# A graph kernel on one core: another order for the four long neighbour lists, and TensorE at two thirds of its clock in the plan

## The chip, the cores and the metric

The kernel runs on one core of one Trainium2 chip. The metric is the device time of one execution in microseconds (us); lower is better. Times inside an execution count from the first instruction of the profiled one.

## The reference, cut to what matters

There are 16 graphs of 1024 nodes with 64 channels and a dense, weighted adjacency matrix each.

```python
# layer 0
h = maximum(layernorm(x), 0)
x = x + matmul(adj / clip(sum(adj, axis=2), 1), h)
# layer 1
h = maximum(layernorm(x), 0)
adj_d = dilate(adj)          # of a node with over 10 neighbours every skip-th one is removed, both ways
for tau, wt in zip([.25, .5, .75], [.25, .5, .25]):       # per node and channel, over h of its neighbours and itself
    agg += wt * interpolated_quantile(h[neighbours(adj_d)], tau)
y = relu((h + agg) @ W1 + b1) @ W2 + b2
x = x + y * mask
```

The numbers of neighbours differ much: a few nodes have many, most have few.

## The kernel before, in words

**Layer 0** takes the 16 graphs one by one: adjacency rows come in by DMA, TensorE transposes them and multiplies, and VectorE (DVE) finds up to 32 neighbours of each row from the signs. Each node's record (channels of layer 1, residual, neighbours) is scattered to the table `srt` of its group, sorted by the number of neighbours. A group is four graphs; there are four groups. `tab` holds a group's channels, `whole` a copy of all groups' tables.

**Layer 1** works on jobs. A job (`Job`) is 128 nodes by T columns whose lists have the same number of places. The lists up to 15 places are the short jobs, by class, of each group (tiles `places`, four buffers). The 512 nodes with the longest lists, 8 of each graph for each of four lengths, are four **long lists** of 128 nodes: 88, 31, 24 and 20 places (`LONG`; called list 88, list 31, list 24, list 20 below). A job goes through these steps:

1. For a long list only, in `long_lists`: its records come by the SP queue (`lS`), GpSimd (POOL) gathers the nodes' adjacency rows (`lat`), and DVE **selects** the neighbours from them: the key of each place, the segments' largest by MAX8 and MATCH_REPLACE8, and from them the row numbers `lidx`.
2. POOL **gathers** one place of 128 nodes at a time by an indirect DMA: `places<-tab,idx` for a short job, `lplaces<-whole,lidx` for a long list. So list 88 takes 88 gathers, list 20 takes 20.
3. The **head**: DVE compares for removed neighbours (`rem`, `gone`, `ok`, `valid`, `q`, `wu`; with an l in front for a long list). `rem` needs all gathers of the job.
4. ScalarE (ACT) adds a huge number to removed places (`places<-places,gone`), one operation a place.
5. DVE **sorts** the places by a network of minima and maxima between `places` and `other` (for a long list between `lplaces` and `long_other`).
6. DVE forms the weights (`w`, `lw`), ACT or DVE multiplies.
7. TensorE (PE) sums the products (`pt`), and the two matrix products of the layer follow over ACT (`ot`, `hid`) and PE (`ps_small`); DVE adds the residual (`y`).
8. POOL scatters the **output** `out_dram<-y`, 128 nodes at a time. For long lists its row numbers are `lnodes_i`; for the short jobs of the last group they are `last_nodes_i`.

List 88 has its own buffer `lplaces0`. The other three lists share two buffers `lplaces`: the third of them can be gathered only when the first has been summed by PE.

**The order.** DVE and POOL are scheduled by hand. Each stream of work is a Python generator that yields before each step what engine it needs and when its inputs are ready by the plan's clocks. `Plan.run` takes the stream that could begin first by these clocks, and among equals the lowest rank. `Plan.note` adds each instruction's cost to the plan's clock of its engine. What `Plan.run` chose is written into the engine's queue, and the engine then follows that queue in order. The loop over the long lists gives each a rank, so that the first one's gathers come ahead of the next one's:

```python
        for l, K in enumerate(LONG):
...
            job = Job(
                pool, n, 1, keys, idx.unsqueeze(1), node, mask, nodes_i, whole, S, NG,
                *(("lplaces", 2) if l else ("lplaces0", 1)), -600 + l, begin=at(whole),
            )
            plan.add(job.run(), 100 * NG + l)
```

The cost of a matmul in the plan is 0.1 us and 0.88 ns for each column of its output, twice as much for float32. All instructions of the plan are recorded by one helper, so the profile gives one line, L228, for nearly all of them; they are told apart by their tiles.

Of the kernel before, what the change touches and what calls it, by code (L numbers as in the profile page):

```python
# [39 lines left out]
LONG = (88, 31, 24, 20)  # L40
# [179 lines left out]
class Timed:  # L220


    def __init__(self, plan, name, engine):
        self._plan, self._name, self._engine = plan, name, engine
# [9 lines left out]
class Plan:  # L234
# [4 lines left out]
    def __init__(self, nc):  # L239
        names = {"vector": "DVE", "scalar": "ACT", "tensor": "PE", "gpsimd": "POOL", "sync": "SP"}  # L240
        self.nc = SimpleNamespace(
            **{attr: Timed(self, name, getattr(nc, attr)) for attr, name in names.items()}
        )
        self.clock = dict.fromkeys([*names.values(), "DMA"], 0.0)
        self.ready, self.used, self.users = {}, {}, {}
        self.slots, self.streams = {}, []
        self.last = self.own = None
        self.parts = set()

    def tile(self, pool, shape, dtype, name, bufs, users=0):  # L250

        res = pool.tile(shape, dtype, name=name, bufs=bufs)
        self.slots.setdefault(name, []).append(res.tensor.name)
        self.users[res.tensor.name] = users
        return res
# [12 lines left out]
    def at(self, *tiles):  # L268
        return max(self.ready.get(t.tensor.name, INF) for t in tiles)

    def note(self, engine, op, args, kwargs):
        if self.own is not None:
            self.clock[engine] = max(self.clock[engine], self.own)
        out = kwargs["out"] if "out" in kwargs else args[0]
        rest = [*args[0 if "out" in kwargs else 1:], *(v for k, v in kwargs.items() if k != "out")]
        rest = [getattr(v, "ap", v) if type(v).__name__.startswith("Indirect") else v for v in rest]
        rest = [v for v in rest if isinstance(v, bass.AP)]
        size = max(math.prod(v.shape[1:]) for v in (out, *rest[:2]))
        start = max(
            self.clock[engine],  # L280
            *(self.ready.get(v.tensor.name, 0.0) for v in rest if self.own is None),
            self.used.get(out.tensor.name, 0.0) if self.own is None else 0.0,
        )
        after = 0.15
        apart = engine == "SP" and out.tensor.name in self.parts
        if apart:
            start = max(self.clock[engine], *(self.ready[v.tensor.name] for v in rest))
        if engine == "DVE":
            half = op == "tensor_tensor" and all(v.dtype == HF for v in (out, *rest))
            time = 0.04 if op == "memset" else 0.07 + size * (0.57e-3 if half else 1.04e-3)  # L290
        elif engine == "ACT":
            pointers = sum(isinstance(kwargs.get(k), bass.AP) for k in ("bias", "scale"))
            time = 0.06 + size * 0.86e-3 + 0.11 * pointers + 0.09 * ("accum_out" in kwargs)
        elif engine == "PE":
            time = 0.1 + math.prod(out.shape[1:]) * 0.88e-3
            if op == "matmul" and rest[0].dtype == F32:
                time *= 2
        elif engine == "POOL":
            time, after = (1.27, 2.2) if op == "indirect_dma_start" else (0.15, 0.1)
            self.last = None  # L300
        else:
            start = max(start, self.clock["DMA"])
            busy = math.prod(out.shape) * 4 / 165e3

            time, after = 0.05, 2.2 + busy * (1 if 4 * out.shape[-1] >= 512 else 2)
            self.clock["DMA"] = start + busy
        self.clock[engine] = end = start + time
        if not apart:
            self.ready[out.tensor.name] = end + after
        for v in rest:  # L310
            self.used[v.tensor.name] = max(self.used.get(v.tensor.name, 0.0), end + after)
        if "accum_out" in kwargs:
            self.ready[kwargs["accum_out"].tensor.name] = end + after
        return start
# [22 lines left out]
def kernel(  # L337
# [27 lines left out]
    with tc.manual_schedule(engines={mybir.EngineType.DVE, mybir.EngineType.Pool}):  # L365
        list_path(tc, x, adj, nodemask, w1, b1, w2, b2, out, go)
# [7 lines left out]
def list_path(ctx, tc, x, adj, nodemask, w1, b1, w2, b2, out, go):  # L374
# [7 lines left out]
    NG = len(GROUPS)  # L382
# [101 lines left out]
    whole = dram.tile([B * TS, W], F32, name="whole")  # L484
# [11 lines left out]
    plan = Plan(nc)  # L496
    plan.parts.update(tab.tensor.name for tab in tabs)
    nc = plan.nc
    new, free, room, at = plan.tile, plan.release, plan.room, plan.at
# [739 lines left out]
    def long_lists(pool):  # L1239
# [1 line left out]
        yield "DVE", always  # L1241
        rev = new(pool, [P, N], HF, "rev", 1)
        nc.vector.tensor_scalar(rev, col_f, -1.0, float(N), op0=OP.mult, op1=OP.add)
        for l, K in enumerate(LONG):
            n = K + 1
            yield "SP", always
            S = new(pool, [P, 1, RW], F32, "lS", 4)
# [62 lines left out]
            for e in range(2):  # L1310
# [7 lines left out]
            yield "DVE", lambda: 0.0 if progress["groups"] == NG else INF  # L1318
            job = Job(
                pool, n, 1, keys, idx.unsqueeze(1), node, mask, nodes_i, whole, S, NG,  # L1320
                *(("lplaces", 2) if l else ("lplaces0", 1)), -600 + l, begin=at(whole),
            )
            plan.add(job.run(), 100 * NG + l)

    progress = {"batches": 0, "begun": 0, "groups": 0, "ahead": 0, "jobs": [0] * (NG + 1)}
    for g in range(NG - 1):
# [1 line left out]
    with tc.tile_pool(name="lay0", bufs=2) as pool:  # L1328

        for stream, first in (  # L1330
            (endings, 0), (channels, 1), (products, 2), (transposes, 4), (listing, 5),
            (beginnings, 6), (loads, 7), (signs, -15),
        ):
            now = [0]
            plan.add(stream(pool, now), lambda first=first, now=now: 10 * now[0] + first)
        plan.run(lambda: progress["batches"] == B)
    with tc.tile_pool(name="long", bufs=1) as pool:

        plan.add(group(NG - 1, pool, "last_"), -2000)
        plan.add(long_lists(pool), -1500)  # L1340
        plan.run()
# [292 lines left out]
```

## Time and profile before

| | |
|---|---|
| median of 3 runs | 1513.86 us (1511.95 to 1516.6) |
| the profiled execution | 1512.82 us, of which its span 1511.0 |
| DVE busy | 1191.3 us, 79% of the span |
| POOL busy | 957.2 us, 63% |
| ACT busy | 816.4 us, 54% |
| PE busy | 738.8 us, 49% |
| gathers of long lists | 163, 1.03 us each |
| last record of layer 0 scattered | at about 889 us |

A busy share is an average over the whole execution, in which layer 0 and layer 1 overlap until about 889 us. For the part after that the stretches of the profile are to be read. POOL's gathers are counted busy while their DMA is prepared, not during the short pause to the next, so a full POOL queue shows as some 75%.

### The profile page before, as it was taken

Reading aid. Unit: us, or ns where it says so; the run is one execution under the profiler, and the core shown is the slowest. Engines: PE = TensorE matmul, PEld = TensorE weight load, DVE = VectorE, ACT = ScalarE, POOL = GpSimd, SP = SyncE. Lnnn points to the kernel's source line nnn. Section 1 sums busy time; section 2 is a strip of 40 time slices with the busy share of each in tenths; the row PEclk is TensorE's granted clock in tenths of the full one; section 3 lists DMA queues with packets and bytes.
Section 4 is the critical chain, followed back from the end, with each engine's and each line's share of the span. In section 5 each row is a group of like instructions: output and inputs, shape, how many; then the busy total and the mean of one; then the engine's idle time right before and its main releaser. Section 6 shows DMA issues by size and latency. Waiting matters only on the chain. (4 is left out here: it accounts for less than half of the span.)

```text
span 1511.0 us, 15983 instructions
## 1 busy us (share of the span) xinstructions
PE 738.8 (49%) x3192; PEld 464.7 (31%) x3192; DVE 1191.3 (79%) x4104; ACT 816.4 (54%) x2789; POOL 957.2 (63%) x1154
## 2 busy tenths in 40 slices
PE   4778777327877556567667620024000123228542
PEld 2434334214544233343444320012000122216432
DVE  6777798997899779859869869893059999986875
ACT  7989878557879457757975520201050223148341
POOL 0122227777678757757777787667777777765083
PEclk8889888658888777869688755555555565558765
DMA  5445665424355253355341242111111111211010
GB/s 177 150 142 168 163 210 160 123 73 114 101 162 152 59 174 94 99 126 161 94 140 31 60 101 68 50 37 28 30 26 23 28 28 40 44 33 22 2 25 13
DMA packets 135718, 133.36 MB, mean 88 GB/s; under 512 B 100756, under 2 KB 103444, under 8 KB 135492
## 3 DMA queue, kind: packets, MB, share of 16 engines
q1 hardware_dynamic: 102876, 90.79, 20.8%
q0 software_dynamic: 32736, 41.47, 11.2%
q14 instruction: 78, 0.64, 0.1%
q8 instruction: 28, 0.46, 0.1%
HBM read 112.90 MB, written 23.61 MB: 90 GB/s over the span
## 5 line engine op out<-in xcount | busy, mean ns | idle before, releaser
L228 POOL DMA_INDIRECT places<-tab,idx x372 | 370.2, 995 | 131.7 <-issue 101.8
L228 PE MATMUL pt<-ident,prod 128*128 128x128 f32 (+1 forms) x736 | 160.2, 377 | 517.8 <-DVE prod L228 241.2
L228 PEld LDWEIGHTS pt<-ident,prod 128*128 128x128 f32 (+1 forms) x736 | 129.3, 256 | 550.4 <-ACT prod L228 412.4
L228 PE MATMUL ps_small<-att,h 128*65 128x512 f32 x512 | 254.7, 644 | 27.3 <-ACT h L228 10.5
L228 POOL DMA_INDIRECT srt<-row,to x128 | 125.9, 984 | 165.8 <-ACT row L228 144.0
L228 PE MATMUL pt<-ident,at 128*128 128x128 f32 x1024 | 176.7, 320 | 96.0 <-ACT att L228 71.1
L228 POOL DMA_INDIRECT lplaces<-whole,lidx x163 | 167.2, 1026 | 55.6 <-issue 48.5
L228 DVE MAX8 rec<-sg 128x8 f16<-128x256 f16 x512 | 180.1, 414 | 4.4
L228 PEld LDWEIGHTS pt<-ident,at 128*128 128x128 f32 x1024 | 136.9, 164 | 143.5 <-ACT att L228 93.8
L228 ACT ACTIVATE sg<-at 128x1024 f16<-128x1024 f32 x128 | 134.8, 1054 | 75.0 <-DMA at<-in_adj_dram 65.7
L228 ACT COPY att<-pt 128x512 f32<-128x512 f32 x256 | 141.9, 582 | 20.7 <-PE pt L228 18.8
L228 POOL DMA_INDIRECT places<-tab,last_idx x124 | 123.8, 998 | 41.3 <-issue 35.0
L228 PEld LDWEIGHTS ps_small<-att,h 128*65 128x65 f32 x512 | 74.7, 151 | 161.9 <-issue 123.2
L228 ACT ACTIVATE places<-places,gone 128x64 f32<-128x64 f32 x496 | 123.5, 335 | 0.5
L228 ACT ACTIVATE prod<-places,w 128x64 f32<-128x64 f32 x213 | 54.1, 336 | 120.5 <-DVE w L228 120.5
L228 POOL DMA_INDIRECT out_dram<-y,nodes_i x93 | 91.8, 987 | 22.6 <-issue 15.1
L228 DVE TENSOR_TENSOR sg<-sg,keyed 128x1024 f16<-128x1024 f16 x128 | 87.2, 681 | 23.7 <-ACT sg L228 23.7
L228 ACT ACTIVATE gone<-gone 128x15 f32<-128x15 f32 (+9 forms) x40 | 8.2, 206 | 169.2 <-DVE ok L228 169.0
L228 DVE TENSOR_TENSOR long_other<-lplaces 128x512 f32<-128x512 f32 (+5 forms) x124 | 64.1, 555 | 29.1 <-ACT lplaces L228 28.9
L228 DVE TENSOR_TENSOR other<-places,other 128x64 f32<-128x64 f32 (+6 forms) x204 | 69.6, 341 | 5.9
L228 PE MATMUL ps_small<-ot,w_sb 128*128 128x128 f32 (+3 forms) x112 | 47.6, 513 | 44.2 <-DVE y L228 31.2
L228 DVE TENSOR_TENSOR places<-places,other 128x64 f32<-128x64 f32 (+2 forms) x208 | 62.3, 309 | 4.9
(231 smaller groups left out, 1670.8 us busy)
## 6 DMA issues: line engine op xcount, KB each, us to landing
at<-in_adj_dram SPq DMA_DIRECT2D x128, 512.0 KB
places<-tab,idx POOLq DMA_INDIRECT x372, 2.5
whole<-tab SPq DMA_DIRECT2D x4, 1057.0 KB
tab<-row SPq DMA_DIRECT2D x16, 264.0 KB
xt<-in_x_dram SPq DMA_DIRECT2D x16, 256.0 KB
lplaces<-whole,lidx POOLq DMA_INDIRECT x163, 2.4
srt<-row,to POOLq DMA_INDIRECT x128, 2.7
places<-tab,last_idx POOLq DMA_INDIRECT x124, 2.4
```

The source lines that it names most:

```text
L228: ins = getattr(self._engine, op)(*args, **kwargs)
```

## The change

There are two edits. The long lists are taken in the order 31, 24, 88, 20, and rank follows that order; which buffers a list uses stays (list 88 has `lplaces0`, the others share two). And from the end of layer 0 on, the plan counts each PE instruction 1.5 times as long. Neither edit alters what an instruction computes; both alter the clocks and ranks by which the plan orders the queues after layer 0.

```diff
@@ Plan.__init__
         self.parts = set()
+        self.pace = 1.0
@@ Plan.note
             if op == "matmul" and rest[0].dtype == F32:
                 time *= 2
+            time *= self.pace
@@ long_lists
-        for l, K in enumerate(LONG):
+
+        for nth, l in enumerate((1, 2, 0, 3)):
+            K = LONG[l]
             n = K + 1
...
-                *(("lplaces", 2) if l else ("lplaces0", 1)), -600 + l, begin=at(whole),
-            )
-            plan.add(job.run(), 100 * NG + l)
+                *(("lplaces", 2) if l else ("lplaces0", 1)), -600 + nth, begin=at(whole),
+            )
+            plan.add(job.run(), 100 * NG + nth)
@@ list_path, after layer 0
         plan.run(lambda: progress["batches"] == B)
+    plan.pace = 1.5
     with tc.tile_pool(name="long", bufs=1) as pool:
```

Written out, POOL's queue before has, from the selection of the lists on: the gathers of list 88 with 14 outputs in it, then those of lists 31 and 24 (55), short jobs and outputs, the output of list 88, the gathers of list 20, and outputs. In the changed kernel it has: the gathers of list 31 with 4 outputs in it, those of list 24, those of list 88 with the outputs of lists 31 and 24 in it, those of list 20 with 10 outputs, then short jobs and outputs; the outputs of lists 88 and 20 stand among the last 23.

## The prediction

> **What bounds the kernel now.** I read the slices first, then the stretch that they point to, then what ended each wait there, and last the end of the chain.
>
> ```profile
> DVE  6777798997899779859869869893059999986875
> ...
> POOL 0122227777678757757777787667777777765083
> ```
>
> One digit is 37.8 us. Layer 0 is over at about 890 us, in the 24th slice. POOL (GpSimd) stays at 7: a gather runs 0.94 us and the next starts 0.30 us later, so 7 is a full queue. DVE (VectorE) has one hole, the digits 3 and 0. Table by stretch, DVE being the third pair of columns and POOL the fifth:
>
> ```profile
> 1032.00:1046.00 14.00, 14.00 (x50) 8.96 (x48) 0.08 (x1) 5.68 (x19) 10.49 (x12) 0.58 0.12 27
> 1048.00:1096.00 48.00, 0.00 (x0) 0.00 (x0) 0.00 (x0) 0.00 (x0) 37.90 (x52) 0.50 0.12 29
> 1096.00:1120.00 24.00, 0.00 (x0) 0.00 (x0) 6.42 (x18) 22.10 (x91) 18.20 (x20) 0.50 0.13 27
> 1120.00:1347.00 227.00, 41.08 (x176) 32.48 (x177) 220.00 (x708) 44.92 (x175) 174.42 (x176) 0.55 0.16 33
> ```
>
> DVE does nothing for 48 us while POOL issues 52 entries; then it is busy 97% of 227 us. What ended the hole, and the other long waits from 1000 us on (us in total, times, longest):
>
> ```profile
> POOL out_dram L228 <- DVE y L228: 58.1, 5, 36.2
> ...
> DVE lrem L228 <- DMA lplaces<-whole,lidx: 50.1, 2, 48.9
> ...
> DVE long_other L228 <- ACT lplaces L228: 28.9, 9, 5.7
> ...
> DVE other L228 <- ACT places L228: 13.6, 3, 11.2
> ```
>
> lrem is the first operation on the list of 88; it needs all 88 gathers. The 36.2 us are POOL waiting at 1390.8 to 1427.0 with the output of list 88, and the gathers of list 20 stand behind it:
>
> ```profile
> 1427.05 0.96 POOL L228 DMA_INDIRECT out_dram<-y,lnodes_i  x1 [36.23 <-DVE y L228]
> 1434.22 0.97 POOL L228 DMA_INDIRECT lplaces<-whole,lidx  x1 [6.22 <-PE pt L228]
> ```
>
> In the timeline DVE then sorts list 31 (1394.4 to 1425.4), 24 (1436.0 to 1461.5) and 20 (1470.5 to 1491.2), and nothing comes after. So POOL's gathers bound the stretch to 1096.5, and VectorE's work, with short waits, the rest. TensorE is never the bound here.
>
> **What the Trainium skill says.** PSUM — Partial Sum Buffer, section Engine vs sequencer instructions: the queues of ScalarE, VectorE and GpSimd are strict FIFO. The trace agrees: twenty gathers of list 20 stood behind one output for 36.23 us. SBUF — State Buffer, section Who interferes with whom: a VectorE instruction with two SBUF inputs contends with a GpSimd instruction that reads SBUF. The trace agrees in sign: with VectorE idle the gathers of list 88 start every 1.25 us, while VectorE sorts list 88 (1119 to 1172) 36 of them take 53 us, 1.50 each; with short jobs between, 1.32 (1172 to 1250).
>
> **The change, part by part.** Both parts alter only the order in which the plan writes the queues. Against the kernel before, the queues are the same up to the selection of the first long list (916.3), no instruction but 26 products on ACT in place of two on DVE (about 2 us) and two memsets is added or removed, so what counts is what stands before what. With the new list order alone the GpSimd queue differs from the changed one only in places of outputs (those of lists 31 and 24 stand up to three gathers elsewhere); the clock part is priced at 0, within 4 us. In SP's queue the copy of the last table to `whole` stands three loads earlier; it still starts when the marks are written (927.2 now) and lands before the first long gather (945): 0.
>
> *Selection, up to 1007.* DVE selects 31 first (20.4 us by its rows, from 916.3) and then 24 (19.9). The row of list 24 lands 4.6 us after its issue at 941.4, so DVE starts it at 946.0 and ends at 965.9. The row for list 88 is issued at 966.1; with 5.8 us of small work before it, its selection (35.6) ends at 1007.3. Only then can the row of list 20 be gathered, and POOL, in order, has done all that stands before it at 998.6: it waits 8.9 us. Before, it waited 4.5 and 3.9 at the two like places.
>
> *The gathers, 1007 to 1160.* After that row 114 entries of POOL's queue lead to the last gather of list 88: 22 of list 24, 88 of list 88, one each of lists 20 and a short job, the outputs of 31 and 24. Meanwhile DVE has 20's selection (19.6), two short rests (7.2), list 31 (30.4), 11 us of waiting on ACT as before 1436.0, and list 24 (25.2, ending 1106). At 1.29, 1.33, 1.43, 1.25 and 1.40 us an entry these stretches take 18, 5, 21, 9 and 18 entries (1.43 and 1.40 I chose between the 1.50 above and the 1.35 of 1434 to 1461); the other 42 go at 1.25. From 1008.8 that ends at 1159, and lrem of list 88 starts at **1160.5 in place of 1096.5: 64 us later.** With all at 1.25 it is 1153, with all at 1.39 1169. Neither output should stop POOL: 31's is ready at 1106 and met at about 1116, 24's at 1118 and met at 1137.
>
> *What DVE no longer has after it.* Lists 31 and 24 now lie in front: 31.0 + 25.5 us of the timeline above and 2.5 for their heads, the 59 us that the rows of both queues also differ by. **Minus 59.** So the hole is not filled, it moves: DVE waits from 1106 to 1118 for the output of list 24, which stands ahead of lrem in its queue, and then to 1160 for the gathers, because nothing else has been gathered. The first of these waits costs nothing while the second covers it.
>
> *The middle.* List 88 waits for the first additions on ACT as it does now (17.6 us in five pieces behind 88 additions in 21.1 us). Between it and the end of 88's sort DVE has 17.5 us more of short jobs, which are missing after it: 0. Short jobs' gathers have 4 us or more of slack by the same entries (the closest: 20 gathers of a job needed at 1361, done at 1357); with four buffers for them I leave 2 us for misses. End of sort: 1160.5 + 250.8 + 17.5 + 2 = 1431.
>
> *The tail.* Before, DVE waited after that point 5.1 + 0.8 + 11.2 + 1.6 + 6.0 + 0.7 + 1.3 + 5.7 = 32.4 us. Now ACT has 18 products of a short job, 67 multiplications of list 88, 17 additions and 12 products of short jobs, then the 20 additions of list 20, at 0.24 each, with copies between: some 38 us (ACT's own rows), against 13 us of DVE's work until list 20. By their order in the queues DVE waits 3.5 and 5.5 us before short jobs and 16.2 before list 20: 25. **Minus 7.** Then list 20 sorts for 19.9. After its weights, 10.3 us passed to the last output's data (1491.2 to 1501.5), and one scatter. Now 15 outputs stand behind the same point, at 1.26: 19 us, which cover the 10.3. **Plus 8.**
>
> Sum by differences: 64 - 59 + 2 - 7 + 8 = +8. Counted forward along the new queues: 1431 + 13 of work + 25 of waits + 20 for list 20 + 20 for its weights and the outputs + 8 from the last scatter to the end (as 1503.0 to 1511.0 now) = 1517, +6. The two differ by roundings of the durations; I take the second, whose steps are the measured rows. The profiled execution took 1512.8 with a span of 1511.0 (1.8 around it), and the median of the runs is 1.0 above it: **1520**.
>
> **The rivals.**
> - *A, the hole moves (0.58):* as above, 1520; by the paces of a gather and 3 us either way in the tail 1509 to 1531.
> - *B, ScalarE drains in time (0.22):* the tail is where it is decided. If list 88's multiplications run while DVE still sorts short jobs, the 25 us shrink to 5: 1500, faster. It decides from 11 us on. For it: before 1347 ACT is busy only 45 of 227 us. Against it: the multiplications need weights formed after the sort, as at 1347.3, and their 16 us belong ahead of list 20 in the queue.
> - *C, an output or a buffer stops POOL (0.20):* as the 36.23 us did. A place is the eleven outputs ahead of the 20-gather job, or the wait for one of four short-job buffers; each 10 us that a job's gathers come late beyond the 4 us of slack reach DVE, which has only list 88 to turn to, and whose queue is fixed. Two such waits: 1540.
> - *That it doesn't do what it says* can be only in part: the order of lists is in the queues; the clock's factor could be without effect, which is already inside A.
>
> **How the numbers follow.** A difference under 0.3% (4.5 us) can't be told from none here. A gives slower 0.36, same 0.19, faster 0.03; B faster 0.20, same 0.02; C slower 0.20. Together faster 0.23, same 0.21, slower 0.56. The range takes B's 1500 as its low end and C's 1540 as its high end; beyond lies under 2 in 10.
>
> **What would show it.** In the changed profile: POOL waiting 9 us for the row of list 20 near 1000; list 31 sorted from about 1040; lrem of list 88 at 1153 to 1169 after a wait of 35 to 45 us on its gathers; end of list 88's sort near 1431; DVE waiting on ACT additions before list 20; a row of some 15 outputs at the very end. Wrong would be lrem before 1145, a VectorE without that wait, or a POOL wait over 10 us in front of gathers after 1160.

## The result

The changed kernel took **1520.71 us** (median of 15 runs, 1516.99 to 1528.16) against 1513.86 us of the kernel before in the same rounds: a ratio of 1.0041, 95% interval 1.0027 to 1.0056. The profiled execution took 1520.98 us with a span of 1519.2. So the change makes the kernel slower, by about 7 us, 0.4%.

The experiments ran on four chips. On two of them, called A and B below, the kernel before took 1956 and 1977 us; on the other two, C and D, 1516 and 1517. Times are therefore compared only with the kernel before on the same chip, or as stretches inside one trace.

### The profile page after: what moved, and what is told of

It reads as the page before. It is cut to its first block, busy times and chain, and to the rows that moved or that the text cites. A ratio compares the mean times of both kernels' runs of the same rounds, so it can differ in the third digit from the quotient of the medians.

```text
span 1519.2 us, 15998 instructions
## 1 busy us (share of the span) xinstructions
PE 764.0 (50%) x3192; PEld 478.7 (32%) x3192; DVE 1189.4 (78%) x4102; ACT 824.0 (54%) x2815; POOL 958.9 (63%) x1152
## 5 line engine op out<-in xcount | busy, mean ns | idle before, releaser
L228 PE MATMUL pt<-ident,prod 128*128 128x128 f32 (+1 forms) x736 | 169.2, 392 | 498.2 <-ACT prod L228 295.0
L228 PEld LDWEIGHTS pt<-ident,prod 128*128 128x128 f32 (+1 forms) x736 | 136.6, 269 | 533.7 <-ACT prod L228 407.7
L228 PE MATMUL ps_small<-att,h 128*65 128x512 f32 x512 | 262.7, 661 | 27.6 <-ACT att L228 10.1
L228 POOL DMA_INDIRECT lplaces<-whole,lidx x163 | 163.5, 1003 | 49.7 <-issue 48.4
L228 POOL DMA_INDIRECT places<-tab,last_idx x124 | 127.5, 1029 | 57.2 <-issue 35.0
L228 ACT ACTIVATE prod<-places,w 128x64 f32<-128x64 f32 x239 | 60.5, 336 | 86.1 <-DVE w L228 86.0
L228 DVE TENSOR_TENSOR long_other<-lplaces 128x512 f32<-128x512 f32 (+6 forms) x124 | 63.9, 554 | 40.1 <-ACT lplaces L228 25.5
L228 ACT COPY ot<-pt 128x128 f32<-128x128 f32 (+3 forms) x56 | 22.0, 394 | 110.9 <-PE pt L228 109.2
```

Source lines behind the costliest of these rows:

```text
L228: ins = getattr(self._engine, op)(*args, **kwargs)
```

## The profile after

The slices of the changed kernel, one digit being 38.0 us:

```profile
DVE  6877698997899779869769867999710899999842
POOL 0122227777677767757776787657777876577714
```

The hole of VectorE is still there. Before it was the digits 3 and 0, in the 28th and 29th slice; now it is 7, 1 and 0 in the 29th to 31st. The last slices of VectorE are 8, 4 and 2 and those of POOL 7, 1 and 4: at the end the two wait for each other.

The table by stretch (busy us and number of instructions of PE, PEld, DVE, ACT, POOL, then the granted clock, the DMA share and GB/s). I cut it at the landmarks of the trace: the wait for list 88's gathers, list 88's sort with short jobs in it, the time to list 20's weights, and the rest.

```profile
1116.00:1161.00 45.00, 0.00 (x0) 0.00 (x0) 0.02 (x1) 0.00 (x0) 34.03 (x37) 0.53 0.13 29
1161.00:1429.00 268.00, 62.74 (x243) 47.44 (x244) 242.90 (x773) 82.22 (x324) 195.11 (x208) 0.54 0.14 31
1429.00:1486.00 57.00, 44.28 (x250) 34.94 (x249) 31.25 (x123) 38.37 (x154) 12.63 (x20) 0.77 0.03 8
1486.00:1519.00 33.00, 13.63 (x72) 11.79 (x72) 3.40 (x17) 5.62 (x21) 15.95 (x29) 0.60 0.06 18
```

In 45 us VectorE does one instruction. Then it is busy 91% of 268 us, and in the 57 us to list 20's weights only 55%. In the last row, 33 us, little but outputs is left.

What ended the long waits from 1000 us on (us in total, times, longest):

```profile
POOL out_dram L228 <- DVE y L228: 49.1, 3, 34.1
...
DVE lrem L228 <- DMA lplaces<-whole,lidx: 45.1, 1, 45.1
...
DVE long_other L228 <- ACT lplaces L228: 25.5, 8, 7.8
...
DVE long_other L228 <- PE pt L228: 14.4, 1, 14.4
...
POOL places L228 <- ACT prod L228: 11.4, 2, 11.1
```

The wait of lrem is 45.1 us where it was 48.9. The wait of 14.4 stands before list 20's sort. The end of POOL's timeline:

```profile
1487.17 0.95 POOL L228 DMA_INDIRECT out_dram<-y,last_nodes_i  x1 [34.12 <-DVE y L228]
...
1495.43 0.96 POOL L228 DMA_INDIRECT out_dram<-y,lnodes_i  x1 [5.93 <-DVE y L228]
...
1510.58 0.95 POOL L228 DMA_INDIRECT out_dram<-y,last_nodes_i  x1 [0.19 <-POOLq L370]
```

Fifteen outputs stand in this row. The first starts when VectorE has come past list 20's sort, two are issued, then POOL waits 5.93 us for the output of list 88, and it and the last twelve follow at 1.26 us each.

## The experiments

The theory was the prediction's: POOL's gathers set when list 88 can start, VectorE and its waits set the rest, and the clock part is worth about nothing. The main rival was that the clock part has a cost of its own.

### The new list order alone

```diff
-    plan.pace = 1.5
+    plan.pace = 1.0
```

It ran on three chips: A, B and D.

> The new list order alone, the plan's clock for TensorE unchanged. Theory of the prediction (the hole moves from 1048-1096 to 1116-1161, the clock part is worth 0 within 4 us): lrem of list 88 within 3 us of 1161 after a wait of about 45 us, list 88's sort done at about 1429, time 1520.7 within 4 us (ratio to before 1.002 to 1.007). Rival (the clock part takes back or adds much): over 5 us away from 1520.7. Rival (the order is worth nothing, the clock part made the change): 1513.9.

> The new list order alone once more; on the first chip the kernel before took 1956 us in place of 1514, with pauses of up to 42 us on ACT, DVE and PE that no wait explains, so the size of the effect could not be read there. If this chip is like the one of the changed kernel (before at about 1514): lrem of list 88 within 3 us of 1161 after a wait of about 45 us, list 88's sort done at about 1429, 1520.7 within 4 us. Rival (the clock part takes back or adds much): over 5 us away from 1520.7.

> The new list order alone, on a chip on which before takes about 1516 (if it is the last one again). Theory: lrem of list 88 within 3 us of 1161 after a wait of about 45 us, list 88's sort done at about 1429, ratio to before 1.0033 as the whole change, within 0.003; so the clock part is worth 0 within 4 us. Rival: the order alone costs the 0.8 to 1.0% that it cost on the two other chips (1528 to 1531), and the clock part gives a part of it back.

On D it took 1514.17 us against 1517.13 of before: **0.9986, interval 0.9974 to 0.9997**. So on this chip the new order alone costs nothing, and gains at most a quarter of a per cent. Neither expectation for the time held: the theory had 1.0033 within 0.003, the rival 0.8 to 1.0% more. On A the ratio was 1.0076 (1.0048 to 1.0105) and on B 1.0097 (1.0065 to 1.0129); those chips are taken up below. On D the hole is where it was foretold:

```profile
1160.74 0.34 DVE L228 TENSOR_TENSOR lrem<-lplaces,lS 128x176 f32<-128x176 f32 x1 [44.56 <-DMA lplaces<-whole,lidx]
```

List 88's weights (`lw`) are done at 1428.2 and list 20's at 1486.0, in the changed kernel at 1429.1 and 1485.9. Up to there the two kernels are the same within 1 us. The difference comes after it. The end of POOL's timeline with the order alone:

```profile
1485.81 0.96 POOL L228 DMA_INDIRECT out_dram<-y,last_nodes_i  x1 [37.53 <-DVE lw L228]
...
1495.90 0.96 POOL L228 DMA_INDIRECT out_dram<-y,lnodes_i  x1 [0.19 <-DVE y L228]
...
1503.47 0.96 POOL L228 DMA_INDIRECT out_dram<-y,last_nodes_i  x1 [0.19 <-POOLq L370]
```

Here too fifteen outputs follow, but the two of long lists (`lnodes_i`) are the ninth and tenth, and the row runs without a stop: 14 steps of 1.26 us from 1485.8 to 1503.5. In the changed kernel the first of them is the third, its data isn't ready, and it stops the row for 5.93 us; the row also begins 1.4 us later. That is the 7.1 us between the two last scatters (1510.6 and 1503.5), and the two spans differ by as much: 1519.2 and 1512.1.

### The changed kernel once more

> The changed kernel itself once more, on the chip of these runs. If this chip is like the first (before at about 1514): 1521 within 3 us. If it is like the two chips on which before took 1956 and 1977 us: theory that the new order of lists makes the whole difference says the ratio to before of e_order and e_order2 there, 1.008 to 1.010. Rival (the clock part adds its own cost there, as e_pace's 1.007 suggests): 1.013 or more. Rival (the two parts give back to each other): 1.005 or less.

On C it took 1521.20 us against 1516.22, ratio 1.0033 (1.0018 to 1.0049), as in the first result. Its trace repeats the first to 0.4 us at every landmark (lrem 1161.3, list 20's weights 1486.3, last scatter 1511.0). So the cost of the whole change is about 0.4%, that of the order alone is none, and the difference, some 7 us, belongs to the clock part. The changed kernel and the order alone were not run beside each other on a chip like C or D; that the two traces agree within 1 us up to list 20's weights, and part by 7.1 us behind them, is what carries this.

### The clock part alone

The list order is again 88, 31, 24, 20; the factor of 1.5 stays.

```diff
-        for nth, l in enumerate((1, 2, 0, 3)):
+        for nth, l in enumerate((0, 1, 2, 3)):
```

It ran on A and D.

> The clock part alone, the lists in the old order 88, 31, 24, 20. Theory: nothing moves before 1347, lrem of list 88 stays at about 1096; near the end the gathers of list 20 stand ahead of list 88's output, but they need the buffer that TensorE frees when list 31 is summed (about 1434), so they start at the same time: 1514 within 4 us. Rival (the 36.2 us of POOL behind list 88's output were on the path): they vanish as a POOL wait in front of list 20's gathers and the time falls by 7 us or more, to 1507 or less. Rival (the clock part is what made the whole slower): 1520 or more.

> The clock part alone, old list order. Theory: lrem of list 88 at about 1096 as before, list 20's gathers ahead of list 88's output but held by the buffer until list 31 is summed: within 4 us of before. Rival 1 (the 36.2 us that POOL waited with list 88's output were on the path): 7 us or more less. Rival 2 (as on the slow chip, ratio 1.007): 8 us or more longer.

On A: 1.0071 (1.0045 to 1.0096). On D: 1540.47 us, **1.0154 (1.0135 to 1.0173)**. The theory of no effect fell, and so did rival 1; rival 2, 8 us or more longer, held. List 20's gathers now stand ahead of list 88's output, and the kernel is 23 us slower. The stop was not removed, only what stands first in it. POOL's timeline on D:

```profile
1448.31 0.97 POOL L228 DMA_INDIRECT lplaces<-whole,lidx  x1 [46.57 <-PE pt L228]
...
1503.34 1.00 POOL L228 DMA_INDIRECT out_dram<-y,lnodes_i  x1 [28.79 <-DVE y L228]
...
1528.66 0.96 POOL L228 DMA_INDIRECT out_dram<-y,last_nodes_i  x1 [0.19 <-POOLq L370]
```

POOL waits 46.57 us for the buffer that TensorE frees when list 31 is summed, and later 28.79 us for a long list's output. Everything behind these two is late, and 21 outputs are left for the end: 20 steps of 1.26 us from 1503.3 to 1528.7. In the kernel before, the last row of outputs goes from 1491.7 to 1502.1:

```profile
1491.70 0.96 POOL L228 DMA_INDIRECT out_dram<-y,lnodes_i  x1 [14.66 <-DVE y L228]
...
1502.09 0.96 POOL L228 DMA_INDIRECT out_dram<-y,lnodes_i  x1 [1.73 <-DVE bad L1346]
```

And VectorE, which before waited for no gathers of a short job between 1347 and list 31's sort, now does:

```profile
1371.20 0.20 DVE L228 TENSOR_TENSOR rem<-places,last_recs 128x36 f32<-128x36 f32 x1 [5.14 <-DMA places<-tab,last_idx]
...
1391.78 0.18 DVE L228 TENSOR_TENSOR rem<-places,last_recs 128x24 f32<-128x24 f32 x1 [6.22 <-DMA places<-tab,last_idx]
...
1398.63 0.17 DVE L228 TENSOR_TENSOR rem<-places,last_recs 128x10 f32<-128x10 f32 x1 [4.82 <-DMA places<-tab,last_idx]
```

List 20's weights are done 11.6 us later than before (1502.9 and 1491.2), of which 3.6 were there already where the selection of the long lists begins (`lnodes`, the row numbers of the first list, at 901.1 and 897.4); the last scatter is 26.6 us later. So about 8 us are VectorE's and 15 the row of outputs. The 23 us between the medians fit these two parts. Why the factor moves the outputs behind is read from the code and not tested further: with a slower TensorE in its clocks the plan takes every output as ready later than it is, and lets gathers that need a long-held buffer pass ahead.

### Twenty more gathers ahead of list 88

```diff
                     gather(A[:, k + 1, t, :], self.table, self.idx[:, t, k:k + 1])
+                    if n == 89 and k == 87:
+                        for e in range(20):
+                            tc.nc.gpsimd.indirect_dma_start(
+                                out=A[:, e + 1, t, :], out_offset=None, in_=self.table,
+                                in_offset=bass.IndirectOffsetOnAxis(ap=self.idx[:, t, e:e + 1], axis=0),
+                            )
```

A first form, on B, issued each of the last 20 gathers twice in a row:

> The changed kernel with the last 20 gathers of list 88 issued twice each, everything else in the same order. Theory (POOL's queue alone sets lrem of list 88, and DVE is busy from there to the end): lrem 20 x 1.25 = 25 us later, at 1186, its wait 70 in place of 45.1 us, and 25 us more in the time, 1545. Rival (there is room behind lrem, in DVE's waits of 31 us in the tail or in the 15 outputs at the end, that takes it in): lrem at 1186 but under 15 us more, below 1536.

There the twin had to wait until the first had landed (1.7 to 2.2 us each time), so it added more than it was meant to: lrem's wait was 82.8 us. It took 2022.99 us, 1.0238 (1.0207 to 1.0268). The second form, on C, is the one of the diff:

> The changed kernel with the gathers of the first 20 places of list 88 issued once more behind its last one (in e_extra20 each waited for its twin to land and cost 3 us in place of 1.25). Theory (POOL's queue alone sets lrem of list 88, and DVE is busy from there to the end): lrem 20 x 1.25 = 25 us later, its wait 70 in place of 45 us, and 22 to 28 us more in the time than the changed kernel has on the same chip. Rival (there is room behind lrem, in DVE's waits in the tail or in the 15 outputs at the end, that takes it in): lrem later by as much, but under 15 us more in the time.

It took 1549.13 us against 1521.20 of the changed kernel on the same chip, 27.9 us more; ratio to before 1.0223 (1.0196 to 1.0250).

```profile
1187.92 0.34 DVE L228 TENSOR_TENSOR lrem<-lplaces,lS 128x176 f32<-128x176 f32 x1 [69.20 <-DMA lplaces<-whole,lidx]
```

The wait grew from 45.05 to 69.20 us, by 24.15: 1.21 us for each gather. Counted from `lnodes` of list 31, which was 2.6 us later in this trace, lrem is 24.1 us later, list 20's weights 23.8 and the last scatter 23.6. **All of it arrives at the end**. Of the rest of the 27.9 us, 2.6 are the later start and 1.7 lie behind the last scatter (10.3 us to the end of the span instead of 8.6). The rival, room in the tail that takes it in, is out. What POOL does ahead of lrem is paid in full.

### Without list 88's multiplications on ACT

```diff
                             if n == 89:
+                                plan.note("ACT", "activation", (src, src), {"scale": w[:, k, t:t + 1]})
+                                continue
```

> The changed kernel without the 67 multiplications of list 88 by its weights on ACT (left out: list 88's places are summed unweighted), everything else in the same order. Theory of the prediction (ACT's rows set the waits of the tail): 67 x 0.24 = 16 us of ACT work go from ahead of list 20's additions; DVE's 14.4 us before list 20's sort fall to under 3, the sort begins at about 1451 in place of 1465.2, and the time falls by 8 to 14 us, to 1507 to 1513. Rival (the wait is for TensorE's sums, as the record names it, or the end is set by POOL's outputs): the wait stays over 8 us, or it goes and the time falls by under 4 us.

It ran on B, beside the first form of the twenty gathers, which has the same order of queues and keeps the multiplications. The plan still counts the work that is left out, so the queues keep their order. VectorE before list 20's sort, first with them, then without:

```profile
1962.85 0.83 DVE L228 TENSOR_TENSOR long_other<-lplaces 128x512 f32<-128x512 f32 x2 [14.17 <-ACT lplaces L228]
```

```profile
1921.04 0.69 DVE L228 TENSOR_TENSOR long_other<-lplaces 128x512 f32<-128x512 f32 x1 [4.20 <-ACT ot L228]
```

From list 88's weights to list 20's weights it was 57.2 us with and 46.1 without; to the last scatter 82.4 and 71.1. The 57.2 is also what the changed kernel shows on C (57.0), so this stretch can be compared across the chips. **Some 11 us of the tail were ACT's multiplications.** To the end of the span it is 13 us (92.7 and 79.7), but 1.7 of these lie behind the last scatter, and the kernels with added gathers have them on C as well. VectorE's wait fell to 4.20 us, not under 3 as expected; the rival, a wait for TensorE's sums that stays over 8 us, is out. The 14.40 us in the changed kernel's two traces, put down to PE `pt`, are the same wait: two other traces with this order (14.17 on B, 11.53 on C) name ACT's additions, and in the changed kernel's own trace these additions run from 1461.05 to 1465.9, while list 20's sort begins at 1465.24:

```profile
1461.05 4.87 ACT L228 ACTIVATE lplaces<-lplaces,lgone 128x64 f32<-128x64 f32 x20
...
1465.24 0.83 DVE L228 TENSOR_TENSOR long_other<-lplaces 128x512 f32<-128x512 f32 x2 [14.40 <-PE pt L228]
```

The ratio to before, 0.9994 (0.9976 to 1.0012), can't be read alone, since the changed kernel itself didn't run on B.

### The kernel before without outputs among list 88's gathers

14 outputs stand in the middle of list 88's gathers in the kernel before, ahead of the last ten. Here they give way until all gathers of list 88 are issued. In POOL's queue they then stand right behind these (1080.5 to 1098), still ahead of the gathers of lists 31 and 24, and not behind those too, as both expectations say.

```diff
@@ in the stream of gathers
+            if n == LONG[0] + 1:
+                progress["hold"] = 1
             for t in range(T):
...
+            if n == LONG[0] + 1:
+                progress["hold"] = 0
@@ rank of an output
+            if progress["hold"]:
+                return 5000
```

> The kernel before, with the 14 outputs that stand in the middle of list 88's gathers put behind the gathers of list 88, 31 and 24. Theory (POOL's queue alone sets lrem of list 88, then DVE is busy to the end): 14 x 1.25 = 17.5 us less in front of lrem, so 1079 in place of 1096.5, and the time falls by about the same less up to 5 us lost at the tail, to 1497 to 1502. Rival (what follows is bound by POOL as a whole, so that an entry moved behind is paid for later): lrem at 1079 but the time within 5 us of 1513.9.

> The kernel before, with the 14 outputs that stand in the middle of list 88's gathers put behind the gathers of lists 88, 31 and 24. Theory (POOL's queue alone sets lrem of list 88, then DVE is busy to the end): 14 x 1.25 = 17.5 us less in front of lrem, so 1079 in place of 1096.5, and the time falls by 10 to 17 us, ratio 0.989 to 0.993. Rival (what follows is bound by POOL as a whole, so that an entry put behind is paid for later): lrem at 1079 but the time within 5 us of before; the ratio 0.997 on the slow chip, where no gain at lrem showed, speaks for it.

On D: 1492.78 us against 1517.13, **0.9841 (0.9821 to 0.9862)**, which beats both kernels and is more than the theory had foretold. The start of list 88, first in the kernel before, then here:

```profile
1096.53 0.34 DVE L228 TENSOR_TENSOR lrem<-lplaces,lS 128x176 f32<-128x176 f32 x1 [48.89 <-DMA lplaces<-whole,lidx]
```

```profile
1081.96 0.34 DVE L228 TENSOR_TENSOR lrem<-lplaces,lS 128x176 f32<-128x176 f32 x1 [31.26 <-DMA lplaces<-whole,lidx]
```

lrem is at 1082.0 in place of 1096.5, and counted from `lnodes` (901.0 and 897.4) 18.2 us earlier: 14 outputs at 1.25 are 17.5. List 20's weights come 17.8 us earlier and the last scatter 19.8, to which the same 3.6 have to be added. So the gain at lrem reaches the end, with 3 to 5 us more behind it, and the rival (an entry put behind is paid for later) is out. Later entries stand differently too (list 88's output starts at 1400.5 in place of 1427.0), and what gives the 3 to 5 us was not tested.

On A the same kernel gained only 0.3% (0.9968, 0.9955 to 0.9982). There lrem had no wait for gathers at all. VectorE's instruction before it was what came late:

```profile
1398.67 0.86 DVE L228 SCALAR_TENSOR_TENSOR y<-ps_small,recs,y 128x64 f32<-128x64 f32 x4 [57.83 <-PE ps_small L228]
```

It waited 57.83 us, put down to TensorE, until 1398.7, and lrem starts 2 us behind it. Gathers that are done earlier can't help there.

### A third buffer for list 20

```diff
-                *(("lplaces", 2) if l else ("lplaces0", 1)), -600 + l, begin=at(whole),
+                *(("lplaces", 3) if l else ("lplaces0", 1)), -600 + l, begin=at(whole),
```

> The kernel before, with a third buffer for lists 31, 24 and 20, so that list 20's gathers need not wait until list 31 is summed and follow those of list 24. Theory (the tail's waits before list 20, POOL's 36 us and some 15 to 20 us of DVE's waits on POOL and ACT behind it, are on the path): lrem of list 88 stays at 1096.5, list 20's sort is free to fill DVE's waits after 1390, and the time falls by 10 to 20 us, to 1494 to 1504. Rival (the 20 gathers at 1.25 us, 25 us, come ahead of short jobs' gathers and DVE starves for those): within 5 us of 1513.9 or more.

It ran on A only: 1998.75 us against 1955.96, **1.0216 (1.0193 to 1.0240)**. The expected gain did not come. List 20's gathers were issued by 1489 and its sort no longer waited for them, but the stretch from list 88's weights to list 20's was 199 us, hardly less than the 203 of the hold variant on the same chip, and VectorE waited in it for ACT instead:

```profile
1839.93 0.43 DVE L228 TENSOR_TENSOR other<-places 128x256 f32<-128x256 f32 x1 [47.81 <-ACT places L228]
```

The longest such wait was 31.56 us in the hold variant on this chip, and 12.47 with the clock part alone. In that stretch VectorE has no wait over 0.5 us for a short job's gathers, so the rival's mechanism (VectorE starves for them) did not show. ACT ran slowly there: in the 47.81 us it started most operations ahead of this job 1.40 us apart, and stood still twice for 7 to 8 us without a release that the trace names. What the third buffer itself costs or gains isn't separated from that, and whether it would lose on a chip like C or D wasn't tried. It stays open.

### What was different on chips A and B

The kernel before takes 29 to 31% longer there. Single operations take as long as elsewhere (a gather 0.94 us, a 128x512 minimum 0.69), but ACT often stands still between two of them. Additions on list 88, on B with the order alone:

```profile
1535.65 0.35 ACT L228 ACTIVATE lplaces<-lplaces,lgone 128x64 f32<-128x64 f32 x1 [0.36 <-issue]
1537.04 0.35 ACT L228 ACTIVATE lplaces<-lplaces,lgone 128x64 f32<-128x64 f32 x1 [1.04 <-issue]
1538.44 0.35 ACT L228 ACTIVATE lplaces<-lplaces,lgone 128x64 f32<-128x64 f32 x1 [1.05 <-issue]
1539.84 0.35 ACT L228 ACTIVATE lplaces<-lplaces,lgone 128x64 f32<-128x64 f32 x1 [1.05 <-issue]
1540.54 0.35 ACT L228 ACTIVATE lplaces<-lplaces,lgone 128x64 f32<-128x64 f32 x1 [0.36 <-issue]
```

They start at distances of 0.70 or 1.40 us. The changed kernel does all 88 in 21.1 us, this run took 96.3; five of the seven traces on A and B need 86 to 97 us for them, the other two 35 and 36. The trace names nothing that these waited for ("issue"). Other waits there end in "remote", a release that the profile can put down to no instruction of the trace:

```profile
1187.71 0.58 ACT L228 COPY ot<-pt 128x512 f32<-128x512 f32 x1 [40.37 <-remote]
```

This one is from A, with the order alone. In each of the seven traces on A and B such waits add up to 335 to 380 us on ACT and 107 to 205 us on VectorE; in the seven traces that were not taken on A or B there is not one. Most of the loss, 260 to 290 us, lies ahead of the selection of the long lists (`lnodes` at 1160 to 1188), where the change has no part. The mean granted TensorE clock is a little lower, 0.63 to 0.64 against 0.68 to 0.70. What holds the engines was not found. So the ratios of A and B say little about the change elsewhere: other waits, ACT's among them, have their part there.

## Why the prediction was right, and where it was not

The time was foretold as 1520 and came out at 1520.7. Step by step, in us of the traces (changed kernel; order alone on D):

| step of the prediction | foretold | changed | order alone |
|---|---|---|---|
| POOL's wait for list 20's row | 8.9 | 8.96 | 8.96 |
| lrem of list 88 | 1160.5 | 1161.0 | 1160.7 |
| its wait on gathers | 35 to 45 | 45.1 | 44.6 |
| end of list 88's sort, with its weights | 1431 | 1429.1 | 1428.2 |
| DVE's waits before list 20's sort | 25 | 24.2 | 24.0 |
| list 20's weights | 1489 | 1485.9 | 1486.0 |
| last scatter | 1509 | 1510.6 | 1503.5 |
| span | 1517 | 1519.2 | 1512.1 |

**The hole moves: right, and shown.** Its place, its length and its cause came out as worked out, and the twenty gathers show that lrem carries through to the end one to one. That lrem was met within 0.5 us is in part luck: counted from `lnodes` it moved by 62.1 us and not by 64, and `lnodes` was 2.3 us later than in the trace of the kernel before. That gathers go more slowly beside VectorE's sort was read from the trace, and no run here shows why; the 36 gathers at 1.50 us are those of lists 31 and 24, and 14 of the 52 entries counted in the hole are the short memsets between outputs. **The tail: right in cause.** The wait before list 20's sort is ACT's, 14.4 us for 16.2 foretold, and the trace without the multiplications has 4.2 there.

**The step that failed is the price of the clock part, "0, within 4 us".** It is 7 us with the new order and 23 with the old one. I had compared the two queues and found only outputs elsewhere ("up to three gathers" from their place), and priced an output by its own 1.26 us. That was said of the outputs of lists 31 and 24; list 88's output, which the clock part moves from ninth to third place in the last row, was not priced. What an output costs is what it waits for, with all that is queued behind it: in third place it stops twelve others and the end for 5.93 us. The prediction's end (15 outputs in one row, 20 us and 8 more) is what the order alone does: 26.1 us from list 20's weights to the end of the span.

**The second error has the other sign and hid the first; that the total came within 1 us is luck.** The order alone was priced at +6 to +8 and measured -2 (0.9986). About 5 us of that lie behind lrem: the middle took 267.4 us instead of 270.5, where the 2 us for missed gathers weren't needed, and the end 26.1 instead of 28. The other 3 probably lie ahead of it: in the one trace of the kernel before, the selection begins at 897.4 (`lnodes`), in the six other traces that were not taken on A or B at 899.8 to 902.5, though the queues are the same up to there. A single trace would then have put the starting point 3 us too early; this isn't shown, since the kernel before was traced only once. With both prices right the sum would have been about 1512 for the order (1513.86 times 0.9986) and 1519 with the clock part.

One sign that I had named as proof against the theory did appear: POOL waited 11.09 us for a buffer of a short job ahead of gathers at 1296.7 (with the order alone 5.07). It cost 1 us at most, since list 88's sort ended within 1 us of the kernel with the shorter wait. The limit of 10 us was set too low; the slack was larger than the 4 us that I had counted.

Of the rivals, B (ACT drains in time) is out by the 14.4 us, and C happened in its smaller form, as an output that stops POOL, at the very end, where I hadn't looked for it. That the clock part could be without effect is out as well.

## What to carry to other kernels

When an order of work is changed, look in the long hole for what the queue still holds ahead of the one transfer that ends it: here 14 outputs put behind the gathers gained 24 us, 18 of them at the start of list 88, while a new order of the lists only moved the hole. An entry in an in-order queue costs what it waits for, together with all that stands behind it, so an output near the end is priced by when its data is ready and not by its own length. And a sum of differences against one trace carries that trace's own offset: check a landmark ahead of the change before trusting a difference of 3 us.

## What the hardware showed that I had not expected

The kernel before took 1514 us in the first runs, 1516 and 1517 on C and D, and 1956 and 1977 on A and B, with equal durations of single operations, 335 to 380 us of waits on ACT that end in no instruction of the trace, and in most traces ACT starting its additions at multiples of 0.70 us. Where a gather was issued twice in a row, the second waited 1.7 to 2.2 us, by the trace for the first one's landing, so a doubled pair took 3.9 us and not 2.5. Both were seen only in passing.
